# Two graph layers over 64 graphs: a step table of its own for the first four graphs, turns on PE for graph 1 and the last two transitions, and weight sums on POOL

## The chip, the cores and the metric

The kernel runs on one core of one Trainium2 chip. The metric is the device time of one execution in microseconds (us); lower is better. Most executions of a kernel here lie within 5 us of each other. A run is called fast when it is not over 1.5% above the fastest of its kernel; here that is every run that could be judged. A profile of one execution gives each engine's instructions: PE (matmuls), DVE (vector), ACT (scalar), POOL (GpSimd) and SP, whose queue issues the DMAs.

## The reference, cut to what matters

Each of 64 graphs has 256 nodes with 512 features and a 256 x 256 adjacency.

```python
def reference(x, adj, W, Wv, bv, aw, ab, Wk, bk):            # names shortened
    h = relu(layernorm(x))                                    # layer 0
    agg = einsum('bij,bjf->bif', adj, h) / max(sum(adj, -1), EPS)
    x = x + relu(concat([h, agg], 2) @ W.T)
    h = relu(layernorm(x))                                    # layer 1
    Xw = h @ Wv + bv
    e = leaky_relu((Xw @ aw[:d])[:, None, :] + (Xw @ aw[d:])[:, :, None] + ab, 0.2)
    t = adj * exp(e);  t = t / sum(t, -1)                     # the "transition"
    H = 0; Xk = h
    for k in range(3):
        H = H + Xk @ Wk[k] + bk[k];  Xk = t @ Xk
    return x + relu(H)
```

## The kernel before

A matrix is turned (transposed) before it can be PE's stationary operand. In the kernel before, that goes through DRAM: 32 x 32 blocks are turned on DVE, four DMAs put them into DRAM, one fetches them. A product of 256 x 512 x 1024 is done in seven block products (Strassen's way), so the weights need sums t1 to t4, and each turned h needs four block sums on POOL. One graph passes through these pieces: `prepare` (norm, turn of h and adj), `layer0`, `turn1` (norm, turn of h), `own` and `pair` (seven products each), `transition`, `twice`. A table fixes the order in which the pieces of neighbouring graphs are interleaved; each letter is one step of a piece, and each engine executes its instructions in that order.

```python
def blocks(ht, pool, name, bufs=1):                           # four sums on POOL
    ...
    nc.gpsimd.tensor_add(s1, a21, a22); nc.gpsimd.tensor_sub(s2, s1, a11)
    nc.gpsimd.tensor_sub(s3, a11, a21); nc.gpsimd.tensor_sub(s4, a12, s2)

def seven(a, b, banks, width, name, c12, c22, ...):           # each add: 2 matmuls, 4 PE records
    add(p, a11, b["b11"], True);  nc.scalar.copy(r, p);              yield
    add(p, s2, b["t2"]);  nc.scalar.copy(d, p); nc.scalar.copy(m16, p);  yield
    ...
    add(p, s4, b["b22"]); nc.vector.tensor_add(c12, p, m16);         yield

def first(sp, spp):                    # graph 0 alone: turned on PE, then all of W, then its adj
    ...
    H0T[0] = blocks(flipped_on_pe(h, F, early, spp, "h0t"), early, "h0t")
    weights_l0(w0_sb, sp, spp)
    ANT[0] = flipped_on_pe(scaled(A[0]), N, early, spp, "ant")

TURN = ("EWU NL NEU mUIWL ... MOP")    # for every graph g: L layer0(g), N prepare(g+1), M/m turn1,
                                       # O own(g-1), P pair(g-2), E transition(g-2), U twice(g-3), W weights
LAST = "mEU UE UO ... V"               # the last three graphs
```

## Time and profile before

| what | value |
|---|---|
| time, median of 6 fast runs | 2654.9 us |
| span of the profiled run | 2653.9 us |
| PE busy | 98% |
| PE wait from 120 to 2600 us | none |
| PE waits before 120 us / after 2600 us | 36.4 us / 3.3 us |

Read it so: the middle runs at PE's pitch, so only the two ends can give anything. The lines that say so stand in the prediction. Two more lines from the groups by shape of the kernel before matter later; after the bar they give busy time and the mean of one in ns:

```profile
L219 POOL TENSOR_TENSOR h1t_s<-h1t_s,h1t 128x256 f32<-128x256 f32 x64 | 74.1, 1158 | 5.0
L219 POOL TENSOR_TENSOR h0t_s<-h0t_s,h0t 128x256 f32<-128x256 f32 x64 | 47.7, 745 | 5.0
L184 DVE SCALAR_TENSOR_TENSOR nmr<-mv,rstd 128x2 f32<-128x2 f32 x128 | 53.1, 415 | 103.7 <-POOL rstd L181 103.7
```

The same POOL sum of the same size takes 1158 ns on average in one place and 745 in another. A DVE operation on two numbers per partition (`nmr`), which takes 0.16 us wherever it runs alone, has a mean of 0.415.

### The profile page before, as it was taken

The numbers are of one execution on the slowest core, as the hardware profiler recorded it, in microseconds if no ns is written. First come the engines' busy times: TensorE is split into PE (matmuls) and PEld (weight loads), VectorE is DVE, ScalarE is ACT, GpSimd is POOL, SyncE is SP. The second block draws the span as 40 slices with busy tenths as digits, with TensorE's granted clock in tenths as the row PEclk, the third lists the DMA queues.
The fourth block names the chain that finished last, engine by engine and source line by source line (L and its number), as shares of the span: only waits on it lengthen the run. The fifth ranks groups of instructions, "written<-read, shape, count | busy, mean of one in ns | idle before, by whom it ended". The sixth has DMA issues, their size and how long they took to land.

```text
span 2653.9 us, 23482 instructions
## 1 busy us (share of the span) xinstructions
PE 2609.8 (98%) x6961; PEld 1346.0 (51%) x6962; DVE 1204.9 (45%) x2670; ACT 895.7 (34%) x1803; POOL 509.6 (19%) x780
## 2 busy tenths in 40 slices
PE   6899999999999999999999999999999999999998
PEld 3455555545555555555455455555555554555554
DVE  5544444444444444444444444444444444444433
ACT  2233333333333333333333333333333333333332
POOL 1221122112112111211221121122112112211210
PEclk8999999999999999999999999999999999999999
DMA  6444453444444444444435444444444454444432
GB/s 188 120 122 106 119 117 103 121 120 105 121 109 113 119 112 113 123 101 123 115 103 121 117 110 117 111 112 121 110 114 123 98 124 118 103 121 110 108 75 58
DMA packets 582942, 301.55 MB, mean 114 GB/s; under 512 B 424224, under 2 KB 547360, under 8 KB 582816
## 3 DMA queue, kind: packets, MB, share of 16 engines
q1 hardware_dynamic: 582816, 300.06, 45.9%
q8 instruction: 56, 0.92, 0.1%
q14 instruction: 70, 0.57, 0.1%
HBM read 166.46 MB, written 133.50 MB: 113 GB/s over the span
## 4 chain that ended last, share of the span: by engine, by line
PE 97%; DMA 1%; DVE 1%; ACT 0%; issue 0%; SPq 0%; POOL 0%; DVEq 0%; ACTq 0%; POOLq 0%
PE bank L225 96%; DMA h0t<-dh0t 0%; SPq L205 0%; DMA row<-ds 0%; DMA tt<-dtt 0%; PE tr L103 0%; DVE turned L200 0%; DMA ds<-sj 0%; DMA z<-in_L_gnn_bv_dram 0%; DMA x<-in_x_dram 0%; DVE stats L174 0%; ACT h L186 0%; PE tr L116 0%; DMA dh1t<-turned 0%; PE bank L467 0%
## 5 line engine op out<-in xcount | busy, mean ns | idle before, releaser
L225 PE MATMUL bank<-l_t,h0t_s 128*128 128x512 f32 x768 | 362.4, 595 | 4.2 <-ACT bank L237 4.2
L225 PE MATMUL bank<-l_t,h1t_s 128*128 128x512 f32 x768 | 360.6, 592 | 0.7 <-ACT bank L237 0.7
L237 ACT COPY bank<-bank 128x512 f32<-128x512 f32 (+1 forms) x192 | 95.9, 499 | 714.4 <-PE bank L225 714.4
L200 DVE STREAM_TRANSPOSE turned<-h 128x512 f32<-128x512 f32 x254 | 180.3, 710 | 312.8 <-ACT h L186 311.9
L218 POOL TENSOR_TENSOR h0t_s<-h0t 128x256 f32<-128x256 f32 x64 | 54.2, 847 | 1032.7 <-DMA h0t<-dh0t 936.1
L225 PE MATMUL bank<-l_b,h0t 128*128 128x512 f32 x512 | 243.8, 599 | 6.0 <-DMA h0t<-dh0t 5.3
L225 PE MATMUL bank<-q,tt 128*128 128x512 f32 x512 | 240.2, 592 | 2.6 <-DMA tt<-dtt 2.6
L225 PEld LDWEIGHTS bank<-l_t,h0t_s 128*128 128x128 f32 x768 | 146.2, 191 | 189.2 <-issue 174.3
L225 PE MATMUL bank<-l_b,h1t 128*128 128x512 f32 x512 | 240.5, 592 | 0.0
L225 PE MATMUL bank<-u,tt 128*128 128x512 f32 x512 | 240.4, 592 | 0.0
L225 PE MATMUL bank<-q,ant 128*128 128x512 f32 x512 | 230.2, 592 | 0.0
L179 POOL TENSOR_SCALAR ve<-mv 128x2 f32<-128x2 f32 x128 | 28.3, 221 | 1005.6 <-DVE mv L175 1005.4
L186 ACT ACTIVATE h<-x,nmr,rstd 128x512 f32<-128x512 f32 x256 | 202.4, 818 | 31.5 <-DVE nmr L184 29.6
L225 PE MATMUL bank<-l1s_t,h1t_s 128*128 128x258 f32 x768 | 198.6, 381 | 0.5 <-ACT bank L237 0.5
L225 PEld LDWEIGHTS bank<-l_t,h1t_s 128*128 128x128 f32 x768 | 145.0, 189 | 104.8 <-issue 92.7
L225 PEld LDWEIGHTS bank<-l1s_t,h1t_s 128*128 128x128 f32 x768 | 146.3, 191 | 102.0 <-issue 83.9
L317 DVE SCALAR_TENSOR_TENSOR x<-bank,x 128x512 f32<-128x512 f32 x128 | 88.3, 691 | 195.2 <-PE bank L225 195.2
L253 DVE TENSOR_TENSOR q<-bank,m 128x512 f32<-128x512 f32 x128 | 88.5, 691 | 191.6 <-PE bank L225 190.6
L174 DVE BATCH_NORM_STATS2 stats<-x 128x6 f32<-128x512 f32 x256 | 172.0, 672 | 5.1 <-DMA x<-in_x_dram 5.1
L225 PEld LDWEIGHTS bank<-l_b,h0t 128*128 128x128 f32 x512 | 101.5, 199 | 127.8 <-issue 120.3
L225 PEld LDWEIGHTS bank<-q,tt 128*128 128x128 f32 x512 | 100.5, 196 | 122.5 <-issue 112.3
L225 PEld LDWEIGHTS bank<-q,ant 128*128 128x128 f32 x512 | 100.4, 196 | 119.4 <-issue 110.3
(100 smaller groups left out, 3228.6 us busy)
## 6 DMA issues: line engine op xcount, KB each, us to landing
x<-in_x_dram SPq DMA_DIRECT2D x64, 512.0 KB, 5.5
dh1t<-turned SPq DMA_DIRECT2D x256, 128.0 KB, 2.8
h1t<-dh1t SPq DMA_DIRECT2D x64, 512.0 KB, 3.9
out_dram<-o SPq DMA_DIRECT2D x64, 512.0 KB, 3.2
dh0t<-turned SPq DMA_DIRECT2D x252, 128.0 KB, 2.8
h0t<-dh0t SPq DMA_DIRECT2D x63, 512.0 KB, 4.2
a<-in_adj_dram SPq DMA_DIRECT2D x64, 256.0 KB, 3.2
dtt<-turned SPq DMA_DIRECT2D x256, 64.0 KB, 3.3
```

The source lines that it names most:

```text
L174: nc.vector.bn_stats(stats[:, c, :], src[:, c, :])
L179: nc.gpsimd.tensor_scalar(ve, mv[:, :, 1], LN_EPS, None, op0=ALU.add)
L186: nc.scalar.activation(to[:, c, :], src[:, c, :], AF.Relu, bias=nmr[:, c : c + 1], scale=rstd[:, c : c + 1])
L200: nc.vector.transpose(self.turned.rearrange("p b r c -> p c b r")[:, c], src.rearrange("p c (b s) -> p c b s", s=Q)[:, c])
L218: nc.gpsimd.tensor_add(s1, a21, a22)
L225: nc.tensor.matmul(ps, lhs, rhs, start=start, stop=stop, skip_group_check=True)
L237: nc.scalar.copy(r, p)
L253: nc.vector.tensor_add(c22, p, m167)
L317: nc.vector.scalar_tensor_tensor(x1[:, c, :], banks0[1 + c], 0.0, x[:, c, :], op0=ALU.max, op1=ALU.add)
```

## The change

Its intent is to fill PE's idle start. Graphs 0 and 1 enter side by side, in banks of their own, both turned on PE (`second` is new); the first four graphs have a table `FIRST`; layer 1's weights are loaded and summed within it; some weight sums move from DVE to POOL. At the end, the last two transitions are turned on PE in place of DRAM.

```diff
-    def combine(b, b12):
-        nc.vector.tensor_sub(b["t1"], b12, b["b11"]) ...            # t1, t2, t3, t4 on DVE
+    def combine(b, b12, eng=(nc.vector,) * 4):
+        for e, to, x, y in zip(eng, ("t3", "t1", "t2", "t4"), ...):
+            e.tensor_sub(b[to], ...)
 ...
+        sums = combine(B1, b12, (nc.gpsimd,) * 4)                   # layer 1
         for c in range(FC):
+            next(sums)
             for s in range(2):
                 nc.vector.scalar_tensor_tensor(scr, wv_sb[c // 2][:, c % 2, :], 1.0, aw_sb[:, s, :], ...
 ...
-    def transition(g):
+    def transition(g, tr_banks=None):
 ...
+        if tr_banks:
+            TT[g] = flipped_on_pe(t, N, tr_banks, work, "tt")
+        else:
             flip = Flip(N, "tt") ...
 ...
+        sums = combine(B0, b12, (nc.gpsimd,) + (nc.vector,) * 3)    # layer 0: t3 on POOL
+        for _ in range(3):
+            next(sums)
+        yield
+        next(sums)
+        yield
+        ANT[0] = flipped_on_pe(scaled(A[0]), N, tr_banks, early, "ant")
+    def second(tr_banks):
+        h = yield from norm_relu(X[1])
+        t = flipped_on_pe(h, F, tr_banks, work, "h1t", 2)
+        yield
+        H0T[1] = blocks(t, work, "h1t", 2)
+        yield
+        ANT[1] = flipped_on_pe(scaled(A[1]), N, tr_banks, early, "ant")
 ...
-    TURN = ("EWU NL NEU mUIWL ...
+    TURN = "EU NL NEU mUIL ...                                      # the same without W
+    FIRST = ("F IIWWA SSA FA SSA FSSA QB QA B QA QQB A QQA ISB aB aQWB QaWB QaWaB WB "
+        "aQWIC bWC bWRC aC bWRaC bWC bWC "
+        "bIORC bROPC ROP RcOP RcbOP RcOP RcOOE cRP cRP "
+        "EDo cDo NEEDo EENDo cEDo NEDo NDoo eNEDk INeDk EdeNzU deNU eUkU kUdk dkNeUkp NeNp edkIp Nep dIp dp p ")
-    LAST = "mEU UE UO UO U UO P O EEP O EEP O EEP OOO eP E eP P u ue ueu eu uep ep ep ep ep p p V V V V V V"
+    LAST = "mEU UE UO UO U UO EEP O EEP O EP OEP OOO eP eP P u uee ue ue u ue up ep p p p p p V V V V V V"
```

More of the change, by code (lines that the diff above doesn't have):

```diff
@@ L1 @@
+import itertools
 from contextlib import ExitStack
@@ L58, in gnn_two_layers @@
     small = ctx.enter_context(tc.tile_pool(name="small", bufs=4))
+    work = ctx.enter_context(tc.tile_pool(name="work", bufs=1))
+    psum = ctx.enter_context(tc.tile_pool(name="psum", bufs=1, space=bass.MemoryType.PSUM))
+    banks0 = [psum.tile([P, F], FP, name=f"bank0_{i}") for i in range(3)]
+    banks1 = [psum.tile([P, F], FP, name=f"bank1_{i}") for i in range(3)]
+    banks2 = [psum.tile([P, F], FP, name=f"bank2_{i}") for i in range(2)]
     dram = ctx.enter_context(tc.tile_pool(name="dram", bufs=2, space=bass.MemoryType.DRAM))
@@ L82, in gnn_two_layers @@
     zero = const.tile([P, F], BF, name="zero")
-    def combine(b, b12):
-        nc.vector.tensor_sub(b["t1"], b12, b["b11"])
-        yield
-        nc.vector.tensor_sub(b["t2"], b["b22"], b["t1"])
-        yield
-        nc.vector.tensor_sub(b["t3"], b["b22"], b12)
-        yield
-        nc.vector.tensor_sub(b["t4"], b["b21"], b["t2"])
-        yield
-    def weights_l0(w0_sb, sp, spp):
-        b12 = sp.tile([P, FC // 2, F], FP, name="l0_b12")
-        for oc in range(FC):
-            for side in range(2):
-                pt = spp.tile([P, FC, P], FP, name="tr")
-                for k in range(FC):
-                    kc = side * FC + k
-                    nc.tensor.transpose(pt[:, k, :], w0_sb[oc][:, kc * P : (kc + 1) * P], ident)
-                put = nc.scalar.copy if side else nc.vector.tensor_copy
-                for kh, to in enumerate((b12, B0["b22"]) if side else (B0["b11"], B0["b21"])):
-                    put(to[:, :, oc * P : (oc + 1) * P], pt[:, 2 * kh : 2 * kh + 2, :])
-        for _ in combine(B0, b12):
-            pass
@@ L110, in flipped_on_pe, with turned_on_pe @@
-    def flipped_on_pe(src, width, pool, spp, name):
-        t = pool.tile([P, width // P, P, NC], FP, name=name, bufs=1)
+    def combine(b, b12, eng=(nc.vector,) * 4):
+        for e, to, x, y in zip(eng, ("t3", "t1", "t2", "t4"), ("b22", None, "b22", "b21"), (None, "b11", "t1", "t2")):
+            e.tensor_sub(b[to], b12 if x is None else b[x], b12 if y is None else b[y])
+            yield
+    def turned_on_pe(blocks, banks):
+        for i in range(0, len(blocks), FC):
+            pt = next(banks).rearrange("p (k n) -> p k n", k=FC)
+            for k, block in enumerate(blocks[i : i + FC]):
+                nc.tensor.transpose(pt[:, k, :], block, ident)
+            yield pt
@@ new lines, in weights_l0 @@
+    def weights_l0(w0_sb, b12, banks):
+        for side, to in enumerate(((B0["b11"], B0["b21"]), (b12, B0["b22"]))):
+            pts = turned_on_pe([w0_sb[oc][:, (side * FC + k) * P :][:, :P] for oc in range(FC) for k in range(FC)], banks)
+            for oc, pt in enumerate(pts):
+                for kh in range(2):
+                    (nc.scalar.copy if oc % 2 else nc.vector.tensor_copy)(to[kh][:, :, oc * P : (oc + 1) * P],
+                                                                         pt[:, 2 * kh : 2 * kh + 2, :])
@@ L113, in flipped_on_pe @@
+    def flipped_on_pe(src, width, banks, pool, name, bufs=1):
+        t = pool.tile([P, width // P, P, NC], FP, name=name, bufs=bufs)
         for c in range(NC):
-            pt = spp.tile([P, FC, P], FP, name="tr")
-            for k in range(width // P):
-                nc.tensor.transpose(pt[:, k, :], src[:, c, k * P : (k + 1) * P], ident)
-            (nc.scalar.copy if c else nc.vector.tensor_copy)(t[:, :, :, c], pt[:, : width // P, :])
-        return t
+            for pt in turned_on_pe([src[:, c, k * P : (k + 1) * P] for k in range(width // P)], banks):
+                (nc.scalar.copy if c else nc.vector.tensor_copy)(t[:, :, :, c], pt[:, : width // P, :])
+        return t
@@ L120, in weights_l1, with spare @@
+    def spare(name, bufs=1):
+        return work.tile([P, 2, F], FP, name=name, bufs=bufs).rearrange("p s f -> p (s f)")
     def weights_l1():
-        aw_sb, *wv_sb, b12 = (work.tile([P, 2, F], FP, name=n, bufs=3 if n == "x1" else 1) for n in ("x1", "u", "o", "q1"))
-        b12s = work.tile([P, NC, 2, HW], FP, name="e", bufs=2).rearrange("p c s w -> p (c s) w")[:, : FC // 2, :]
+        aw_sb = spare("x1", 4).rearrange("p (s f) -> p s f", s=2)
+        wv_sb = [work.tile([P, NC, 2, HW], FP, name="e", bufs=2).rearrange("p c s w -> p (c s w)")[:, : 2 * F]
+                 .rearrange("p (c f) -> p c f", c=2) for _ in range(2)]
+        b12s = spare("u")[:, : FC // 2 * HW].rearrange("p (c w) -> p c w", w=HW)
+        b12 = spare("o").rearrange("p (c f) -> p c f", f=F)
@@ L126, in weights_l1 @@
         scr, bv_sb = (work.tile([P, F], FP, name=n) for n in ("z0", "z1"))
-        biases = [work.tile([P, F], FP, name=n) for n in ("m16_1", "m167_1", "tt")]
+        two = work.tile([P, FC, P, NC], FP, name="h1t", bufs=2).rearrange("p k n c -> p (k n c)")
+        biases = [two[:, :F], two[:, F:], work.tile([P, F], FP, name="tt")]
         vc = small.tile([P, 2, FC], FP, name="vc", bufs=1)
@@ L131, in weights_l1 @@
         src = [wk[k].rearrange("(h c p) o -> h p c o", p=P, h=2) for k in range(NW)]
-        nc.sync.dma_start(aw_sb.rearrange("p s f -> p (s f)"), bcast(aw, 0, 2 * F))
+        nc.sync.dma_start(aw_sb, bcast(aw, 0, 2 * F))
         for h in range(2):
             nc.sync.dma_start(wv_sb[h], wv.rearrange("(h c p) o -> h p c o", p=P, h=2)[h])
-        yield
         halves = ((b12s, 0, 1), (B2["b22"], 1, 1), (B2["b11"], 0, 0), (B2["b21"], 1, 0))
@@ L142, in weights_l1 @@
             nc.sync.dma_start(to, src[k][kh])
+        nc.sync.dma_start(bv_sb, bcast(bv, 0, F))
+        nc.sync.dma_start(ab_sb, bcast(ab, 0, 1))
+        for k in range(NW):
+            nc.sync.dma_start(biases[k], bcast(bk, k * F, F))
         yield
+        sums = combine(B1, b12, (nc.gpsimd,) * 4)
         for c in range(FC):
+            next(sums)
             for s in range(2):
@@ L150, in weights_l1 @@
             nc.vector.tensor_copy(to[:, :, half], vc[:, col, 2 * kh : 2 * kh + 2])
-        yield
         yield from combine(B2, b12s)
-        nc.sync.dma_start(bv_sb, bcast(bv, 0, F))
-        nc.sync.dma_start(ab_sb, bcast(ab, 0, 1))
-        for k in range(NW):
-            nc.sync.dma_start(biases[k], bcast(bk, k * F, F))
-        yield
         for s in range(2):
@@ L161, in weights_l1 @@
         nc.vector.scalar_tensor_tensor(c0, cc[:, 0:1], cc[:, 1:2], ab_sb, op0=ALU.add, op1=ALU.add)
-        yield
-        yield from combine(B1, b12)
         nc.vector.tensor_add(bk_sb, biases[0], biases[1])
@@ L166, in weights_l1, with finished, norm_relu @@
         yield
-    def norm_relu(src, to):
+    def finished(steps):
+        while True:
+            try:
+                next(steps)
+            except StopIteration as end:
+                return end.value
+    def norm_relu(src):
         stats = small.tile([P, NC, 6], FP, name="stats")
@@ L184, in norm_relu @@
         nc.vector.scalar_tensor_tensor(nmr, mv[:, :, 0], -1.0, rstd, op0=ALU.mult, op1=ALU.mult)
+        h = early.tile([P, NC, F], FP, name="h", bufs=1)
         for c in range(NC):
-            nc.scalar.activation(to[:, c, :], src[:, c, :], AF.Relu, bias=nmr[:, c : c + 1],
+            nc.scalar.activation(h[:, c, :], src[:, c, :], AF.Relu, bias=nmr[:, c : c + 1],
                                  scale=rstd[:, c : c + 1])
             yield
+        return h
     class Flip:
@@ L284, in prepare @@
     def prepare(g):
-        h = early.tile([P, NC, F], FP, name="h", bufs=1)
-        yield from norm_relu(X[g], h)
+        h = yield from norm_relu(X[g])
         flip = Flip(F, "h0t")
@@ L305, in prepare, with layer0 @@
         yield
-    def layer0(g):
-        q = work.tile([P, NC, F], FP, name="q0")
-        yield from seven(H0T.pop(g), B0, banks0, F, "0", q[:, 0, :], q[:, 1, :])
-        steps = spread(banks0[1:], ANT.pop(g), q)
+    def layer0(g, banks=None, name="0"):
+        banks = banks or banks0
+        q = work.tile([P, NC, F], FP, name=f"q{name}")
+        yield from seven(H0T.pop(g), B0, banks, F, name, q[:, 0, :], q[:, 1, :])
+        steps = spread(banks[1:], ANT.pop(g), q)
         next(steps)
@@ L314, in layer0 @@
         next(steps)
-        x, x1 = X.pop(g), work.tile([P, NC, F], FP, name="x1", bufs=3)
+        x, x1 = X.pop(g), work.tile([P, NC, F], FP, name="x1", bufs=4)
         for c in range(NC):
-            nc.vector.scalar_tensor_tensor(x1[:, c, :], banks0[1 + c], 0.0, x[:, c, :], op0=ALU.max, op1=ALU.add)
+            nc.vector.scalar_tensor_tensor(x1[:, c, :], banks[1 + c], 0.0, x[:, c, :], op0=ALU.max, op1=ALU.add)
         X1[g] = x1
@@ L321, in turn1 @@
     def turn1(g):
-        h = early.tile([P, NC, F], FP, name="h", bufs=1)
-        yield from norm_relu(X1[g], h)
+        h = yield from norm_relu(X1[g])
         flip = Flip(F, "h1t")
@@ L334, in turn1, with own @@
         yield
-    def own(g):
+    def own(g, p=None):
         e = E[g] = work.tile([P, NC, 2, HW], FP, name="e", bufs=2)
-        yield from seven(H1T[g], B2, [banks0[0]] + banks2, HW, "s", e[:, 0, 1, :], e[:, 1, 1, :],
+        yield from seven(H1T[g], B2, [p or banks0[0]] + banks2, HW, "s", e[:, 0, 1, :], e[:, 1, 1, :],
                          e[:, 0, 0, :], e[:, 1, 0, :])
@@ L380, in transition @@
         yield
-        flip = Flip(N, "tt")
-        flip.turn(t)
-        flip.put()
-        yield
-        TT[g] = flip.get(work)
+        if tr_banks:
+            TT[g] = flipped_on_pe(t, N, tr_banks, work, "tt")
+        else:
+            flip = Flip(N, "tt")
+            flip.turn(t)
+            flip.put()
+            yield
+            TT[g] = flip.get(work)
         yield
@@ L424, in loads_of, with set_bits, first @@
             yield
-    def first(sp, spp):
+    def set_bits(banks):
+        for bank in banks:
+            nc.tensor.matmul(bank, zero[:, :P], zero, start=True, stop=True)
+    def first(tr_banks):
         load(0, X)
-        w0_sb = [sp.tile([P, 2 * F], FP, name=f"w0_sb{oc}") for oc in range(FC)]
+        w0_sb = [spare(*n) for n in (("x1", 4), ("q1",), ("u",), ("o",))]
         for oc in range(FC):
             nc.sync.dma_start(w0_sb[oc], w0[oc * P : (oc + 1) * P, :])
-        load(0, A)
-        for what in (X, A):
-            load(1, what)
+        for g, what in ((1, X), (0, A), (1, A)):
+            load(g, what)
         make_identity(nc, ident)
@@ L437, in first @@
         nc.gpsimd.memset(zero, 0.0)
-        h = early.tile([P, NC, F], FP, name="h", bufs=1)
-        for _ in norm_relu(X[0], h):
-            pass
-        H0T[0] = blocks(flipped_on_pe(h, F, early, spp, "h0t"), early, "h0t")
-        weights_l0(w0_sb, sp, spp)
-        ANT[0] = flipped_on_pe(scaled(A[0]), N, early, spp, "ant")
-    TURN = ("EWU NL NEU mUIWL NL NNU NEL EWNU EUL ENL ENL EWP WNL L IO MP MO MP WO MP EMO NMP WO WP O WO MOP")
-    LAST = "mEU UE UO UO U UO P O EEP O EEP O EEP OOO eP E eP P u ue ueu eu uep ep ep ep ep p p V V V V V V"
+        set_bits(banks0[1:] + banks1[1:])
+        h = finished(norm_relu(X[0]))
+        H0T[0] = blocks(flipped_on_pe(h, F, tr_banks, early, "h0t"), early, "h0t")
+        b12 = spare("q0").rearrange("p (c f) -> p c f", f=F)
+        weights_l0(w0_sb, b12, tr_banks)
+        sums = combine(B0, b12, (nc.gpsimd,) + (nc.vector,) * 3)
[5 more added lines that the diff above has]
+        ANT[0] = flipped_on_pe(scaled(A[0]), N, tr_banks, early, "ant")
+        yield
+    def second(tr_banks):
+        h = yield from norm_relu(X[1])
+        t = flipped_on_pe(h, F, tr_banks, work, "h1t", 2)
+        yield
+        H0T[1] = blocks(t, work, "h1t", 2)
+        yield
+        ANT[1] = flipped_on_pe(scaled(A[1]), N, tr_banks, early, "ant")
+        set_bits(banks2)
+        yield
+    TURN = "EU NL NEU mUIL NL NNU NEL ENU EUL ENL ENL EP NL L IO MP MO MP O MP EMO NMP O P O O MOP"
+    FIRST = (
+        "F IIWWA SSA FA SSA FSSA QB QA B QA QQB A QQA ISB aB aQWB QaWB QaWaB WB "
+        "aQWIC bWC bWRC aC bWRaC bWC bWC "
+        "bIORC bROPC ROP RcOP RcbOP RcOP RcOOE cRP cRP "
+        "EDo cDo NEEDo EENDo cEDo NEDo NDoo eNEDk INeDk EdeNzU deNU eUkU kUdk dkNeUkp NeNp edkIp Nep dIp dp p "
+    )
+    LAST = "mEU UE UO UO U UO EEP O EEP O EP OEP OOO eP eP P u uee ue ue u ue up ep p p p p p V V V V V V"
     def run(order, pieces):
@@ L457, in gnn_two_layers @@
     with tc.manual_schedule(engines={getattr(mybir.EngineType, e) for e in ("PE", "DVE", "Activation", "Pool", "SP")}):
-        with tc.tile_pool(name="setup", bufs=1) as sp, \
-                tc.tile_pool(name="setup_ps", bufs=3, space=bass.MemoryType.PSUM) as spp:
-            first(sp, spp)
-        work = ctx.enter_context(tc.tile_pool(name="work", bufs=1))
-        psum = ctx.enter_context(tc.tile_pool(name="psum", bufs=1, space=bass.MemoryType.PSUM))
-        banks0 = [psum.tile([P, F], FP, name=f"bank0_{i}") for i in range(3)]
@@ L464, in gnn_two_layers @@
-        banks1 = [psum.tile([P, F], FP, name=f"bank1_{i}") for i in range(3)]
-        banks2 = [psum.tile([P, F], FP, name=f"bank2_{i}") for i in range(2)]
-        for bank in banks0[1:] + banks1[1:] + banks2:
-            nc.tensor.matmul(bank, zero[:, :P], zero, start=True, stop=True)
-        norms, w = {}, weights_l1()
-        for g in range(G):
-            norms[g] = turn1(g)
-            run(TURN, {"I": loads_of(g + 2) if g + 2 < G else iter(()), "N": prepare(g + 1) if g + 1 < G else iter(()),
-                       "L": layer0(g), "M": norms[g], "W": w,
-                       **({"m": norms.pop(g - 1), "O": own(g - 1)} if g > 0 else {}),
-                       **({"E": transition(g - 2), "P": pair(g - 2)} if g > 1 else {}),
-                       **({"U": twice(g - 3)} if g > 2 else {})})
@@ L476, in gnn_two_layers @@
-        run(LAST, {"m": norms.pop(G - 1), "U": twice(G - 3), "E": transition(G - 2), "P": pair(G - 2),
-                   "O": own(G - 1), "u": twice(G - 2), "e": transition(G - 1), "p": pair(G - 1), "V": twice(G - 1)})
+        norms = {g: turn1(g) for g in range(G)}
+        tr_banks = itertools.cycle([banks1[0], *banks2])
+        run(FIRST, {"F": first(tr_banks), "S": second(itertools.cycle(banks2)), "W": weights_l1(),
+                    "I": itertools.chain(*map(loads_of, range(2, 6))), "A": layer0(0), "B": layer0(1, banks1, "1"),
+                    "z": map(set_bits, [[banks1[0]]]), "C": layer0(2), "D": layer0(3), "Q": prepare(2), "R": prepare(3), "N": prepare(4),
+                    "a": norms[0], "b": norms[1], "c": norms[2], "d": norms[3], "O": own(0), "o": own(1, banks1[0]),
+                    "k": own(2), "P": pair(0), "p": pair(1), "E": transition(0), "e": transition(1), "U": twice(0)})
@@ new lines, in gnn_two_layers @@
+        for g in range(4, G):
+            run(TURN, {"I": loads_of(g + 2) if g + 2 < G else iter(()), "N": prepare(g + 1) if g + 1 < G else iter(()),
+                       "L": layer0(g), "M": norms[g], "m": norms[g - 1], "O": own(g - 1), "E": transition(g - 2),
+                       "P": pair(g - 2), "U": twice(g - 3)})
+        tr_banks = itertools.cycle(banks0[1:])
+        run(LAST, {"m": norms[G - 1], "U": twice(G - 3), "E": transition(G - 2, tr_banks), "P": pair(G - 2),
+                   "O": own(G - 1), "u": twice(G - 2), "e": transition(G - 1, tr_banks), "p": pair(G - 1),
+                   "V": twice(G - 1)})
```

## The prediction

> **What bounds the kernel now.** I read the page's busy table and slices first, then busy time by stretches, then the waits of PE, then the chain at the two ends.
>
> ```profile
> span 2653.9 us, 23482 instructions
> PE 2609.8 (98%) x6961; PEld 1346.0 (51%) x6962; DVE 1204.9 (45%) x2670; ACT 895.7 (34%) x1803; POOL 509.6 (19%) x780
> PE   6899999999999999999999999999999999999998
> PEclk8999999999999999999999999999999999999999
> ```
>
> PE is full in all slices but the first two and the last, and the granted clock dips only at the start. The stretches say where the missing time lies:
>
> ```profile
> core 0: us, PE busy (x) PEld busy (x) DVE busy (x) ACT busy (x) POOL busy (x), PEclk, DMA share, GB/s
> 0.00:40.00 40.00, 22.61 (x77) 13.58 (x79) 16.92 (x34) 11.86 (x23) 6.07 (x20) 0.91 0.59 187
> 40.00:80.00 40.00, 28.92 (x65) 13.46 (x63) 23.16 (x56) 7.10 (x13) 12.17 (x16) 0.83 0.68 194
> 80.00:120.00 40.00, 32.12 (x76) 15.89 (x77) 22.56 (x47) 14.38 (x29) 8.46 (x14) 0.87 0.41 103
> 160.00:2500.00 2340.00, 2340.00 (x6249) 1207.79 (x6249) 1068.61 (x2375) 803.55 (x1618) 458.71 (x694) 1.00 0.47 114
> 2600.00:2654.00 54.00, 46.12 (x118) 21.89 (x116) 0.98 0.19 51
> ```
>
> From 120 us to 2600 us PE never waits. A busy PE need not be a fast one, so I also take its pitch, from start to start:
>
> ```profile
> 107.97 3.60 PE L225 MATMUL bank<-q,ant 128*128 128x512 f32 x8
> 111.40 1.03 PE L225 MATMUL bank<-l1s_b,h1t 128*128 128x258 f32 x4
> 112.28 1.02 PE L225 MATMUL bank<-l_t,h1t_s 128*128 128x512 f32 x2
> ```
>
> (111.40 - 107.97) / 8 = 0.429 us for a record 512 wide, (112.28 - 111.40) / 4 = 0.22 for one 258 wide (0.2175 with more digits of other rows). Each f32 matmul leaves two records. The groups by form count 5120 and 1792 of them, so 80 and 28 a graph: 34.3 + 6.1 = 40.4 us a graph, 64 x 40.43 = 2587 us in all. The span is 67 us longer. In the first 120 us the groups hold 124 wide and 44 narrow records, 62.8 us of work: 57.2 us are lost there. The last 54 us lose about 8; the two sum to the 67, nearly. The 57.2 consist of 36.4 us of waits, 10.5 of setup on PE (transposes of graph 0 and the weights, and the matmuls that set the banks' bits) and about 10.4 of matmuls at a reduced clock (73.3 us busy for 62.8 of work). The waits, longest first:
>
> ```profile
> PE tr L116 <- ACT h L186: 9.0, 1, 9.0
> PE bank L225 <- ACT m_s L250: 7.0, 1, 7.0
> PE tr L116 <- ACT an L281: 6.9, 1, 6.9
> PE bank L225 <- DMA h0t<-dh0t: 5.3, 1, 5.3
> PE bank L225 <- ACT bank L237: 4.7, 4, 2.6
> PE bank L225 <- ACT m L250: 2.2, 1, 2.2
> ```
>
> The first 9.0 is the load of x and its norm. The others come from graphs entering one by one: each pass through layer 0, norm, turn in DRAM, load back is serial, and there is no other graph's work for PE. At the tail the chain shows one such wait:
>
> ```profile
> 2613.15 0.72 DVE turned L200
> 2615.25 1.83 DMA dtt<-turned
> 2617.17 5.04 DMA tt<-dtt
> 2622.26 8.97 PE bank L225 x20
> 2631.25 0.58 ACT bank L237
> ```
>
> PE had finished pair of graph 62 at 2619.64 and waited 2.62 us for its turned transition; a bank copy cost another 0.66.
>
> **What the Trainium skill says.** "TensorE: Matmul & The Clock Gate", Part 1: after an idle window of about 3.4 us the PE clock falls to half, and about 3.4 us of sustained work restores it. The trace agrees in kind: after the wait of 5.3 us the next four 512-wide records took 3.78 us instead of 1.88, and the granted clock stayed at 0.50 until about 61 us. After a wait of only 2.24 us, at 101 us, it fell too, a few us later. Part 4 of the same page says a PE transpose gives a full 128x128 turn, lands in PSUM and so needs a copy, and does not count as busy for the clock; the trace has 32 of them in 5.23 us, 0.163 each, and cannot decide on the clock. "DMA: Bandwidth & Descriptors", section "Anatomy of one DMA", gives about 2 us fixed per transfer, mostly the receipt of the last byte (fitted on the GpSimd path). Here four 64 KB puts land in 3.3 us (median) and the 256 KB load in 2.7, or 5.04 at the tail, so a turn through DRAM costs 5 to 9 us. "GPSIMD Engine Reference", "Engine selection", calls elementwise work with two inputs about 2x slower there than on DVE: 0.74 us for 256 elements on POOL against 1.23 for 1024 on DVE agrees, so about 2.9 us (estimate) for a POOL sum of 1024.
>
> **The change part by part.** The built order shows that the repeated table is the old one without the weights' steps; the matmuls of the 64 graphs are the same. The middle should stay at 40.43 us a graph; everything is decided at the ends.
>
> *Start to layer 0.* Load, norm and the 40 transposes keep their times, so PE is at 16.0 us. The turn of adj 0 moves from before layer 0 into it, so the first product starts at 16.0 instead of 26.95. It runs to 17.9; the second needs t2. The weights' copies end at 16.7, then t1 and t2 at 1.23 each: 19.2. t3 went to POOL (16.7 to 19.6) and is not awaited. Products 2, 3, 4 (1.72 each) end at 24.3.
>
> *adj 0 and graph 1 on PE.* DVE does stats of x1, t4, nmr and deg by 23.4; ACT scales adj by 26.0. PE waits about 1.3 us; 12 small turns and their copies through two banks hold it to 28.2. Then six products, three of each graph by turns, so that the copies of one lie under the products of the other, and the spread of graph 0: 6 x 1.72 + 3.43 = 13.7, PE at 41.9.
>
> *adj 1.* DVE reaches deg of adj 1 only after x1 of graph 0, which needs that spread. x1 1.3, deg and reciprocal 1.1, ACT 0.5: the first turn at 44.5. Turns, copies and two bit-setting matmuls: layer 0 of graph 1 resumes at 46.8. By then PE has done ten products and one spread, 17.2 + 3.4 = 20.6: 26.2 us lost. The kernel before ended the same work at about 61.8, with 41.2 lost.
>
> *The rest of the table.* Four products and a spread of graph 1 end at 57.1. Graph 2's turned h went out at about 39 and is back near 50, so it waits for no DMA. Its block sums stand on POOL behind two weight sums of 2.9, so the second product waits about 1.5, and layer 0 of graph 2 ends at 57.1 + 12.0 + 1.5 = 70.6. Own of graph 0 needs its turned h1: h at 57, turned on DVE by 61.7 among the weights' sums, out and in by 71 to 73: 1.5 of wait. Then 21.5 us of own 0, pair 0 and spread 2 and 18.1 of layer 0 of graph 3 with own 1 run without a long wait. Graph 0's transition (sj near 91, row near 102, tt near 118 to 119) meets PE at 118: 1 us. The single pair of graph 1 and the u copies: about 1.3. Sum: 26.2 + 1.5 + 1.5 + 1 + 1.3 = 31.5 us lost to waits, setup and turns.
>
> *Clock.* The first products come after transposes and 2 us of waits, and the hole at 42 to 45 is 3 us: two dips of 3.4 to 7 us at half clock would cost 1.7 to 3.4 each; with part of it under waits I take 3.5 (estimate). Head: 35 us lost against 57.2, so 22 us gained.
>
> *Tail.* Removed: 2.62, and most of the 0.66. Added: 8 transposes, 8 x 0.163 = 1.3. And a new place to wait: PE now reaches the turn of graph 63 near 2629, while the row of sj came at 2626.4, and exp, max, sums and scale took 6.2 us after it. Without the other DMAs the row may come a us or two earlier; I take 1.2 of wait. Net 0.5 us.
>
> Sum: 2655.0 - 22 - 0.5 = 2632.5; I say 2632.
>
> **The rivals.** (a) *Graph 1 starves the weights and flips*: the loads of layer 1's weights now follow x 2 and adj 2 and one reuses the buffer of w0, so it is issued only after 16 us; SP issues in order. 4 MB at the 300 GB/s of the first 40 us is there by 35. For it: DVE is 58% busy in the second stretch already and runs in order. If DVE sums and norms lag 10 us, the gain falls to 12: 2643. (b) *The clock*: if transposes leave PE at half clock until 24 us and each of the small waits trips it, 5 us more: 2637. (c) *All holes filled better than my walk*: only 16 of start, 6 of turns and 4 of copies remain, 26 lost: 2623. (d) *The handover to the repeated table is out of phase* and it waits every graph: 0.5 us each would be 30, back to 2662. The same order ran 2480 us without a wait, so I give this a few per cent.
>
> **Range and chances.** (a) to (c) span 2623 to 2643, the range for 8 in 10. Faster by over 2% would need below 2603, a loss of 6 us in the head, when the first product cannot start before 16: 1%. Slower by over 2% needs (d) doubled: 1%.
>
> **What would show it.** First layer-0 product near 16 us; a PE wait of about 3 us near 42 for adj 1; no wait for h0t from DRAM; full slices from about 125 us with the same pitch; at the tail no wait for tt and a short one before the turn of graph 63. Wrong if waits of PE remain in the middle, if the first 160 us still hold over 50 us of loss, or if the clock is below 0.8 over most of the first 60.

## The result, and the profile after

The changed kernel takes 2643.5 us (median of 6), the one before 2654.9. The ratio is 0.9959, 95% interval 0.9946 to 0.9972: faster, by 11.4 us, well inside 2%. (Ratios here are the mean time of one kernel's fast runs over that of the other's fast runs of the same rounds, so not quite the ratio of the medians quoted.) The predicted time was 2632, with a range of 2623 to 2643; the measured one lies just above it, and the gain is half of the predicted one. The profiled execution is the slowest of the changed kernel's six, 1.9 us above their median, so its trace shows a little less gain than the median does.

The busy table and slices of the changed kernel:

```profile
span 2643.6 us, 23486 instructions
PE 2612.3 (99%) x6983; PEld 1347.6 (51%) x6983; DVE 1204.4 (46%) x2664; ACT 897.2 (34%) x1807; POOL 524.2 (20%) x785
PE   7999999999999999999999999999999999999999
PEclk9999999999999999999999999999999999999999
```

The first stretches, with the columns shown of before (busy us of PE, PEld, DVE, ACT, POOL, then the granted clock):

```profile
0.00:40.00 40.00, 28.33 (x92) 16.27 (x93) 17.17 (x33) 13.29 (x26) 13.81 (x27) 0.96 0.70 256
40.00:80.00 40.00, 31.46 (x67) 13.32 (x67) 31.25 (x59) 9.23 (x16) 17.82 (x14) 0.87 0.35 81
80.00:120.00 40.00, 37.94 (x113) 21.26 (x112) 19.14 (x48) 14.44 (x32) 12.77 (x20) 1.00 0.54 114
120.00:160.00 40.00, 35.80 (x97) 18.75 (x97) 17.01 (x40) 11.86 (x25) 5.10 (x8) 0.96 0.50 122
```

PE is fuller, but from 40 to 80 us it still misses 8.5 us, and DVE is now busy 31.25 of 40 there (some of this will turn out to be waiting). From 160 us on PE never waits until the tail, at the old pitch. What PE waited for (total, times, longest):

```profile
PE bank L240 <- DVE q L275: 7.4, 2, 5.3
PE bank L101 <- ACT h L200: 5.2, 1, 5.2
PE bank L101 <- ACT an L296: 3.5, 2, 2.4
PE bank L240 <- DVE l_t L93: 3.4, 1, 3.4
PE bank L240 <- ACT u L425: 2.3, 1, 2.3
```

Gone are the 9.0 (in part: PE now sets bank bits during the load of x), the 7.0, the 6.9 and the 5.3 for a turn through DRAM. In their place DVE holds PE, for a sum `q` (5.3 and 2.1 us) and for layer 0's weight sum t2 (3.4). The longest wait for each of these, and the one for u's copies, are followed by four records that take 3.6 to 3.8 us in place of 1.88, which is half clock:

```profile
21.69 3.58 PE L240 MATMUL bank<-l_t,h0t_s 128*128 128x512 f32 x4 [3.37 <-DVE l_t L93]
65.04 3.78 PE L240 MATMUL bank<-q,ant 128*128 128x512 f32 x4 [5.30 <-DVE q L275]
137.80 3.57 PE L240 MATMUL bank<-u,tt 128*128 128x512 f32 x4 [2.28 <-ACT u L425]
```

The reason that DVE is late is seen when DVE and POOL are laid side by side. In DVE's order of time (start, length):

```profile
17.05 1.22 DVE L93 TENSOR_TENSOR l_t<-q,l_b 128x1024 f32<-128x1024 f32 x1 [0.28 <-ACT q L110]
18.37 3.17 DVE L93 TENSOR_TENSOR l_t<-l_b,l_t 128x1024 f32<-128x1024 f32 x1
57.40 2.75 DVE L159 SCALAR_TENSOR_TENSOR z<-e,x 128x512 f32<-128x512 f32 x1
60.09 2.28 DVE L197 SCALAR_TENSOR_TENSOR nmr<-mv,rstd 128x2 f32<-128x2 f32 x1
64.31 0.68 DVE L275 TENSOR_TENSOR q<-bank,m 128x512 f32<-128x512 f32 x1
```

And in POOL's:

```profile
17.36 3.10 POOL L93 TENSOR_TENSOR l_t<-l_b,q 128x1024 f32<-128x1024 f32 x1 [2.77 <-ACT l_b L110]
57.25 2.35 POOL L93 TENSOR_TENSOR l_t<-l_b,o 128x1024 f32<-128x1024 f32 x1
59.56 2.79 POOL L93 TENSOR_TENSOR l_t<-o,l_b 128x1024 f32<-128x1024 f32 x1
63.91 1.06 POOL L234 TENSOR_TENSOR h0t_s<-h0t_s,h0t 128x256 f32<-128x256 f32 x1
```

t1 and t2 on DVE are the same operation on the same size: 1.22 us and 3.17. POOL's t3 ends at 17.36 + 3.10 = 20.46; t2 ends 1.08 us after that, as if it had started only then. DVE's product at 57.40 ends 0.55 us after POOL's sum at 57.25 does, and `nmr` at 60.09, otherwise 0.16 us, ends at 62.37, just behind POOL's second sum (62.35). But `q<-bank,m` at 64.31, with one operand in PSUM, takes its usual 0.68 under a POOL sum. So the theory formed: an operation of DVE with two SBUF inputs and one of POOL that reads SBUF exclude each other for their whole length. The Trainium skill says just that, in "SBUF — State Buffer", section "SBUF: two separate sides": the port pair that both share is "an exclusive lock, not a bandwidth split". The prediction had not looked it up.

### The profile page after: what moved, and what is told of

Its sections match the earlier page's. It is cut to its first block, busy times and chain, and to the rows that moved or that the text cites. A ratio compares the mean times of both kernels' runs of the same rounds, so it can differ in the third digit from the quotient of the medians.

```text
span 2643.6 us, 23486 instructions
## 1 busy us (share of the span) xinstructions
PE 2612.3 (99%) x6983; PEld 1347.6 (51%) x6983; DVE 1204.4 (46%) x2664; ACT 897.2 (34%) x1807; POOL 524.2 (20%) x785
## 4 chain that ended last, share of the span: by engine, by line
PE 97%; DVE 1%; issue 0%; ACT 0%; DMA 0%; SPq 0%; POOL 0%; DVEq 0%; ACTq 0%
PE bank L240 97%; PE bank L101 0%; DVE z L159 0%; DVE l_t L93 0%; DMA x<-in_x_dram 0%; DMA row<-ds 0%; DVE turned L215 0%; SPq L220 0%; DVE stats L187 0%; ACT z L377 0%; DVE nmr L197 0%; DVE o L433 0%; ACT an L296 0%; DVE l1s_t L93 0%; POOL rstd L194 0%
## 5 line engine op out<-in xcount | busy, mean ns | idle before, releaser
L240 PE MATMUL bank<-l_t,h1t_s 128*128 128x512 f32 x780 | 367.4, 594 | 0.7 <-ACT bank L252 0.7
L240 PE MATMUL bank<-l_t,h0t_s 128*128 128x512 f32 x756 | 356.9, 595 | 4.1 <-DVE l_t L93 3.4
L240 PE MATMUL bank<-l_b,h0t 128*128 128x512 f32 x504 | 237.2, 593 | 0.0
L240 PEld LDWEIGHTS bank<-u,tt 128*128 128x128 f32 x512 | 100.6, 197 | 121.5 <-issue 88.4
```

The lines of the kernel that those rows point to most:

```text
L240: nc.tensor.matmul(ps, lhs, rhs, start=start, stop=stop, skip_group_check=True)
```

## The experiments

The theory is that the blocking by POOL's sums makes DVE late and that this cost the missing part of the gain. The main rival: DVE is just loaded with too much in the order of the table, and the long operations are a sign and not the cause. Others: the hole for adj 1; the u copies on ACT; the tail. Twelve kernels ran, each beside the kernel before on the same chip.

| run | edits to the changed kernel | us, median | before | ratio | 95% interval |
|---|---|---|---|---|---|
| after_again | none | 2642.8 | 2655.2 | 0.9955 | 0.9943 to 0.9968 |
| t3_on_dve | t3 on DVE | 2644.5 | 2656.5 | 0.9955 | 0.9940 to 0.9970 |
| l1_sums_early | layer 1's POOL sums at 37 us | 2640.0 | 2656.5 | 0.9941 | 0.9927 to 0.9956 |
| l1_sums_on_dve | layer 1's sums on DVE | 2643.6 | 2656.5 | 0.9952 | 0.9935 to 0.9968 |
| adj1_early | scaling of adj 1 earlier | 2640.9 | 2656.5 | 0.9944 | 0.9929 to 0.9959 |
| all_three | t3_on_dve, l1_sums_early and adj1_early | 2634.2 | 2654.2 | 0.9924 | 0.9909 to 0.9939 |
| u_copy_first | u's copies ahead on ACT | 2640.5 | 2654.2 | 0.9948 | 0.9933 to 0.9963 |
| tail_as_before | old tail | 2643.6 | 2654.2 | 0.9961 | 0.9946 to 0.9976 |
| best1 | all_three, u_copy_first, weight products earlier | 2630.9 | 2654.2 | 0.9913 | 0.9897 to 0.9930 |
| unblocked | t3_on_dve and l1_sums_early | 2640.1 | 2655.2 | 0.9940 | 0.9927 to 0.9952 |
| l1_blank | memsets for sums (wrong result) | 2639.0, one run | 2655.2 | - | - |
| best2 | best1, bias sums later | 2628.6 | 2655.2 | 0.9899 | 0.9884 to 0.9914 |

A single edit is worth little more than the spread.

**t3_on_dve.**

```diff
-        sums = combine(B0, b12, (nc.gpsimd,) + (nc.vector,) * 3)
+        sums = combine(B0, b12)                     # rows in the order t1, t2, t3, t4
```

> The changed kernel with one edit: layer 0's weight sum t3 goes from POOL to DVE, behind t1 and t2. Theory (POOL and DVE block each other when both read two SBUF operands): DVE's sum t2, 3.17 us in the changed kernel, is 1.22 again, the second product starts at 19.6 us instead of 21.7 and the wait of 3.37 before it is about 1.3; 2643.5 becomes about 2641.5. Rival (t2 is late because its data come late, and the sum just ran beside much DMA traffic): t2 stays above 2.5 us and the time stays or grows by the 1.2 us of the added DVE sum, 2643 to 2645.

In the trace t2 is 1.21 us again, the second product's wait is 1.42 and it starts at 19.78 us, not 21.69: the theory's half of the expectation holds. The time did not fall, 2644.5. The trace shows why. ACT's scaling of adj 0 is waited for longer (1.93 us, not 1.08), but since the second product now runs at full clock, the lead is still 2.7 us when the turn of adj 0 begins (27.09 us, not 29.80). It is 1.0 us at the product after that (32.38, not 33.40), because the turns of graph 1 and the product behind them now run at half clock:

```profile
28.05 1.57 PE L104 MATMUL bank<-ident,h 128*128 128x128 f32 x8
29.41 3.14 PE L243 MATMUL bank<-l_t,h0t_s 128*128 128x512 f32 x4
```

In the changed kernel these take 1.09 and 1.88 us. The lead is 0.8 us at 64, and own of graph 0 starts at 83.86 instead of 84.22.

**l1_sums_early.** DVE's order and load are untouched; only POOL's sums move, to where POOL was idle.

```diff
-        sums = combine(B1, b12, (nc.gpsimd,) * 4)
+        for _ in combine(B1, b12, (nc.gpsimd,) * 4):
+            pass
+        yield
         for c in range(FC):
-            next(sums)
-        "... FSSA QB QA B QA ..."
+        "... FSSA QB QA W B QA ..."
```

> The changed kernel with one edit: the four weight sums of layer 1 stay on POOL but stand where DVE has no operation with two SBUF inputs (POOL is idle from 37 to 56 us). DVE's order and load are untouched. Theory (blocking): the products for aw on DVE are 0.69 us each instead of 1.31 on average, nmr 0.16 instead of 2.28, PE's wait of 5.30 before the second half of graph 1's spread falls to about 1 and the later one of 2.06 to under 0.5; with less half clock, 2643.5 becomes 2634 to 2637. Rival (DVE is simply loaded with the weights' sums in the order of the table): the waits stay within 1 us of 5.3 and 2.06, the time within 1.5 us of 2643.5.

The same two places of DVE in this kernel's order of time, then PE's wait for `q`:

```profile
57.07 0.69 DVE L160 SCALAR_TENSOR_TENSOR z<-e,x 128x512 f32<-128x512 f32 x1
57.69 0.15 DVE L198 SCALAR_TENSOR_TENSOR nmr<-mv,rstd 128x2 f32<-128x2 f32 x1
```

```profile
59.89 1.99 PE L241 MATMUL bank<-q,ant 128*128 128x512 f32 x4 [0.49 <-DVE q L276]
```

The product is 0.69 us, not 2.75; `nmr` 0.15, not 2.28; PE's wait 0.49, not 5.30, and no half clock follows it. The rival falls for this wait, since DVE's order did not change. The time fell to 2640.0, 3 us short of what was expected. The wait before own of graph 0 did not shrink as expected (2.40 us, since DVE's bias sums stand in front of `q`, as best2 will show), and the waits for tt (1.72) and for u's copies (2.72) grew. Counted from the first product (16.03 us here, 16.44 in the changed kernel), own of graph 0 starts 5.5 us earlier, the second product of graph 1's pair only 4.1 us.

The new place is not as free as the expectation says. Two operations of DVE still wait for POOL's sums there, and the second has only one input in SBUF:

```profile
36.74 2.30 DVE L198 SCALAR_TENSOR_TENSOR nmr<-mv,rstd 128x2 f32<-128x2 f32 x1 [1.13 <-POOL rstd L195]
42.61 1.20 DVE L293 TENSOR_SCALAR deg<-deg 128x2 f32<-128x2 f32 x1
```

Elsewhere they take 0.16 and 0.17 us.

**l1_sums_on_dve.**

```diff
-        sums = combine(B1, b12, (nc.gpsimd,) * 4)
+        sums = combine(B1, b12)
```

> The changed kernel with one edit: the four weight sums of layer 1 run on DVE, at the same places of the table, as in the kernel before. Theory (blocking): before the sum q that PE waits for, DVE gains two sums of 1.22 and loses about 4.85 of blocking, so PE's wait of 5.30 falls to about 2.9; 2643.5 becomes 2640 to 2642. Rival (load of DVE): the two sums are added to the load, the wait grows to about 7.7 and the time to 2645 to 2648.

PE's wait for `q` was 2.71 us: it shrank although DVE got more work, so the blocking cost DVE more than the sums themselves. The time stayed at 2643.6, not the 2640 to 2642 expected. In the trace the other waits for `q` took back half of the 2.6 us (2.61 us before own of graph 0 where the changed kernel has 2.06, and a new one of 0.78), and a product behind them ran at half clock (3.46 us for 1.88, at 83.87). This is the kernel before's choice, and it is no better.

**l1_blank.** A wrong result on purpose (relative error 0.18).

```diff
-        sums = combine(B1, b12, (nc.gpsimd,) * 4)
+        def blank():
+            for to in ("t3", "t1", "t2", "t4"):
+                nc.gpsimd.memset(B1[to], 0.0)
+                nc.gpsimd.memset(B1[to], 0.0)
+                yield
+        sums = blank()
```

> The changed kernel with a wrong result on purpose: in the places of the four POOL sums of layer 1 stand pairs of memsets on POOL of the same targets, which write SBUF and read nothing. If it is the reading of SBUF by both engines that blocks, DVE's products beside them are 0.69 us each and PE's wait of 5.30 is near 1. If any POOL instruction of that length blocks DVE, products beside them stay above 1.3 us and the wait above 3.

DVE and POOL side by side in this kernel:

```profile
57.61 0.69 DVE L164 SCALAR_TENSOR_TENSOR z<-e,x 128x512 f32<-128x512 f32 x1
```

```profile
56.99 0.95 POOL L158 MEMSET l_t<- 128x1024 f32 x1
57.88 0.95 POOL L157 MEMSET l_t<- 128x1024 f32 x1
```

The eight products average 0.679 us and PE waits 0.49. POOL is at work beside the products here too (two memsets of 0.95 us for each sum of 2.35), but with instructions that only write: for DVE's operations with two SBUF inputs it is the reading that blocks. Memsets are not harmless to all of DVE: of its copies of two numbers from SBUF to SBUF behind the products, which take 0.155 us alone, two took 0.98 and 1.60 and ended with POOL's memset at 65.9 us.

**unblocked and after_again.** Both edits for the blocking together, beside the changed kernel itself.

> The changed kernel itself, unaltered, beside the others on the same chip: 2642 to 2645. It sets the scale for the three below, since single runs of one kernel spread by 3 us.

> The changed kernel with both POOL edits (t3 on DVE, layer 1's sums early on POOL), all else as it is: what the blocking costs in all. Theory: the sum of what the two edits gave alone, 3.5 to 5 us, so 2638.5 to 2640; DVE's products 0.69, t2 1.22. Rival (the two hide each other, because own of graph 0 hangs on graph 0's transposes through DRAM): no more than layer 1's sums early alone, and the wait for DVE's q before own of graph 0 grows instead.

2640.1 against 2642.8. The intervals of the ratios overlap, as they share the noise of the kernel before; but the five runs of unblocked (2637.1 to 2641.5) all lie below the five of the changed kernel (2642.0 to 2645.8), and the means differ by 4.2 us. It is no more than l1_sums_early gave alone (ratio 0.9940 against 0.9941), as the rival said. The traces show where it goes. In unblocked own of graph 0 starts at 76.46 us instead of 83.45, and the second product of graph 1's pair comes at 143.71 instead of 147.19. Counted from each run's first product (15.33 and 15.97 us, before any edit acts), the blocking costs 6.4 us where it acts, and 2.8 are left 70 us later. First after_again, then unblocked:

```profile
83.45 1.15 PE L240 MATMUL bank<-l1s_b,h1t 128*128 128x258 f32 x4 [2.06 <-DVE q L275]
84.43 1.88 PE L240 MATMUL bank<-q,ant 128*128 128x512 f32 x4
137.57 1.99 PE L240 MATMUL bank<-u,tt 128*128 128x512 f32 x4 [2.58 <-ACT u L425]
```

```profile
76.46 1.15 PE L244 MATMUL bank<-l1s_b,h1t 128*128 128x258 f32 x4 [2.40 <-DVE q L279]
77.44 3.25 PE L244 MATMUL bank<-q,ant 128*128 128x512 f32 x4
132.42 3.66 PE L244 MATMUL bank<-u,tt 128*128 128x512 f32 x4 [2.88 <-ACT u L429]
```

Both have the same two waits, 0.3 us longer in unblocked. But there each is followed by half clock (3.25 and 3.66 us, not 1.88 and 1.99), which takes most of the 3.5 us that were given back.

**adj1_early.**

```diff
         H0T[1] = blocks(t, work, "h1t", 2)
+        an = scaled(A[1])
         yield
-        ANT[1] = flipped_on_pe(scaled(A[1]), N, tr_banks, early, "ant")
+        ANT[1] = flipped_on_pe(an, N, tr_banks, early, "ant")
```

> The changed kernel with one edit: degree and scaling of adj 1 stand before the norm of graph 2 and the residual of graph 0, where DVE and ACT are idle (32 to 35 us). My walk had a hole there that hangs on DVE's order: the turn of adj 1 then starts right after the spread of graph 0, the wait of 2.37 us vanishes. If nothing downstream hangs on PE here, 2643.5 becomes about 2641; if the time regained is only waited for later, because the spread of graph 1 waits for DVE's sum q anyway, that wait grows by as much and the time stays within 1 us of 2643.5.

The wait of 2.37 us is gone (0.68 remains before the bank bits are set), own of graph 0 starts at 80.34, and the time is 2640.9, as expected. This hole was in the prediction and measured as predicted; it shows only what the table left.

**u_copy_first.**

```diff
-        "... EdeNzU deNU eUkU kUdk dkNeUkp ..."
+        "... EdNzU dNU eUkeU kUdk dkNeeUkp ..."
```

> The changed kernel with one edit: the two copies of u of graph 0 stand on ACT ahead of the exponentials of graph 1, which wait for their row from DRAM. If u's copies were late only because of ACT's order, the wait of 2.28 us at 137.8 and the half clock after it vanish: 2 to 4 us less, about 2640.5. If PE depends on the row anyway soon after, the wait turns up at the next product of graph 1 (q times tt) and the time stays within 1.5 us of 2643.5.

The wait and the half clock behind it vanish, 2640.5. In the changed kernel ACT's exponentials of graph 1, which their row from DRAM lets start only at 134.71 us, and two scalings stood in front of u's copies in ACT's order, up to 137.18, while PE had finished the spread at about 134.5.

**tail_as_before.** The old `LAST`, and both calls of `transition` without `tr_banks`.

> The changed kernel with its last table and its two last transitions as they were in the kernel before (turned through DRAM). It tells the tail's share of the gain: the traces put it at 1.4 us (51.27 us from the first tail product to the last in the kernel before, 49.86 in the changed one). Expected 2644 to 2646, with a wait of 2.6 us for tt back in the tail. My prediction had 0.5.

2643.6, slightly below the range: no difference shows in the time. In the trace the wait for tt is back (2.35 us), and from the first of these tail products to the last the tail takes 51.01 us, against 49.86 in the changed kernel. The turns on PE are worth about 1.2 us, which the run-to-run spread hides. In the changed kernel they are these; the second set was waited for 0.17 us:

```profile
2603.14 0.60 PE L101 MATMUL bank<-ident,an 128*128 128x128 f32 x4
2620.75 0.84 PE L101 MATMUL bank<-ident,an 128*128 128x128 f32 x4 [0.17 <-ACT an L393]
```

**all_three, best1, best2.** First the three edits t3_on_dve, l1_sums_early and adj1_early together; then also u_copy_first, with three pairs of weight products moved into a time when DVE was idle; then the bias sums behind the `q` that own of graph 0 waits for.

```diff
-        "... ISB aB aQWB QaWB QaWaB WB aQWIC bWC bWRC aC bWRaC bWC bWC bIORC bROPC ROP ..."
+        "... ISB aWWWB aQWB QaB QaaB B aQWIC bWC bWRC aC bWRaC bWC bWC bIORC bROPC ROP ..."    # best1
+        "... ISB aWWWB aQWB QaB QaaB B aQWIC bWC bWRC aC bWRaC bC bC bIORC bROPWC ROP ..."     # best2
```

> The changed kernel with the three edits together: t3 on DVE, layer 1's POOL sums early, adj 1 early. Alone they moved the start of own of graph 0 from 84.2 us to 83.9, 78.3 and 80.3. If the head is one chain on which these times stand one behind the other, it starts near 74 and the time falls to 2634 to 2637. If another chain takes over behind them (transition of graph 0 and the row of graph 1, which end in waits for tt and for u's copy), the head's gain is eaten by longer waits there (over 2 us for tt, over 3 us for u) and the time is 2637 to 2640.

> A version meant to beat both: the three edits, u's copies first, and three of the four pairs of weight products on DVE moved to where DVE waited idle (49 to 54 us). If the waits are what the head loses, 2643.5 becomes 2630 to 2635, which is where the prediction had put the change itself; if the transition of graph 0 bounds the head, it stays at 2636 to 2640.

> best1 with one more edit: the bias sums on DVE (3.3 us) stand behind the sum q that own of graph 0 waits for (2.13 us in best1). If that wait was only DVE's order, it falls under 0.7 and the time is 1 to 2 us below best1, near 2629.5. If own of graph 0 waits next for its turned h1 or its block sums, the time stays at 2630 to 2632.

All three are correct and their times fall within what was expected or just below it: own of graph 0 starts at 73.46, 72.93 and 71.97 us. The wait before it falls from 2.13 us in best1 to 0.78 in best2 (under 0.7 was expected), so that wait was DVE's order. best2 beats both kernels, 2628.6 us, 26.6 below the kernel before and 14 below the changed one. PE's waits in its first 160 us, longest in total first:

```profile
PE bank L104 <- ACT h L204: 4.8, 1, 4.8
PE bank L104 <- ACT an L300: 1.9, 1, 1.9
PE bank L244 <- DMA h0t<-dh0t: 1.9, 1, 1.9
PE bank L449 <- POOL zero L461: 1.9, 1, 1.9
```

DVE is no longer among the first; what is left is the load of x and small things.

## Why the prediction was right or wrong

Its frame held. The middle kept its pitch and had no waits; the gain came from the start; it was below 2%; the first product began at 16.44 us, "near 16"; the hole for adj 1 was there (2.37 us, predicted near 3). That graph 2 waited for no DMA before its layer 0 was luck: its turned h was issued at 58.86 us and back 4.0 us later, not near 50, and only since PE itself came late (68.6 us, not 57.1) was it not waited for. best1 and best2, where PE is earlier, wait 1.9 us for it. The size was wrong. The head gained 2594.44 - 2585.60 = 8.8 us (the place of the same first tail product in the two traces) where 22 were predicted, so it loses 57.2 - 8.8 = 48.4 us and not 35. The walk against the trace:

| place | predicted us | measured us | late by |
|---|---|---|---|
| first product | 16.0 | 16.44 | 0.4 |
| second product | 19.2 | 21.69 | 2.5 |
| spread of graph 0 ends | 41.9 | 45.4 | 3.5 |
| layer 0 of graph 1 resumes | 46.8 | 49.70 | 2.9 |
| spread of graph 1 ends | 57.1 | 68.6 | 11.5 |
| own of graph 0 starts | 72.1 | 84.22 | 12.1 |
| graph 0's transition meets PE | 118 | 130.9, after 1.3 of wait | 12.9 |

The step that failed is the durations of DVE and POOL where they run together. "t1 and t2 at 1.23 each: 19.2" took each engine's operation at its length alone; beside POOL's t3, t2 took 3.17. "Four products and a spread of graph 1 end at 57.1" assumed that DVE's `q` comes when PE has finished; it came 5.3 us late, of which the early sums and the memsets show 4.8 to be blocking (0.49 is left without it). The prediction did price the POOL sums, "about 2.9 us (estimate)" for 2.35 measured without a collision, and let a product wait for POOL behind two of them; that they stop DVE was not in it. unblocked puts this step, with the half clock that it brings, at 6.4 us at own of graph 0, of the 12.1, and at 4.2 us of the time, of the 11.5 missing. So it is the largest single step and not the whole. Term by term, the 13.4 us that the head loses beyond the prediction in this trace are: 7.4 at the two places where DVE was late (3.37 us of wait for 1.3, 5.30 for none), 3.1 of half clock, 1.6 at u's copies and the wait of 0.66 us behind them, and about 1.3 in small terms of both signs.

A second term was mis-sized: "The single pair of graph 1 and the u copies: about 1.3" measured 2.28 + 0.66 us of wait and 1.7 more at half clock (four records in 3.57 us instead of 1.88; in after_again none). It does not go with the blocking: the wait is 2.58 us in after_again and 2.88 in unblocked; ACT's order sets it, as u_copy_first shows.

The third is the clock, which was added as 3.5 us and not set into the walk. Three times before own of graph 0 matmuls ran slow: the second product 3.58 for 1.88, the products at 49.7 us 4.89 for 3.60, the spread at 65.04 3.78 for 1.88; 4.9 us, with 1.7 more for u: 6.6 for 3.5. In this trace a wait of 2.3 to 5.3 us brought 1.3 to 1.9 more with it, so a mis-sized wait costs more than itself. Rival (b) fell in its first half, since the first product ran at full speed (1.89 us at 16.44); its second half, that the waits trip the clock, is what happened, at 3.1 us for the 5 it named.

Rival (a), DVE lagging, was nearest: 2643. It was right in its outcome, mostly by luck: its reason, late loads and DVE's share of work in order, is shown only for the wait before own of graph 0 (2.1 us, 0.8 in best2). For the wait of 5.3 it is not: l1_sums_early had the same DVE order and hardly waited for that `q`. Rival (c) was not reached; best2, with 2628.6, is 5.6 us above it. In the tail 0.5 us were predicted and 1.2 to 1.4 found; the wait for graph 63's turn was 0.17 us and not 1.2.

Three readings of the prediction were loose, without consequence for the result. The terms that it names from own of graph 0 to the transition give 111.7 us and not 118; a spread of graph 3 and two products of own of graph 2 (5.2 us) are left out of them, though not out of the table above. The "300 GB/s of the first 40 us" is 187 in its own lines. And the transposes of the kernel before could have decided on the clock: their records last 421 ns at first and 273 later.

What stays open: how much of the half clock after the waits belongs to an edit and how much to the single execution that was profiled. Executions of one kernel differ here. In the trace of tail_as_before the second product ran at full speed after the same wait of 3.37 us, and in after_again the u product did after 2.58 us; each is worth 1.7 us.

## What to carry to other kernels

Moving an operation to an idle engine is free only if the engines share nothing: before giving POOL a sum over SBUF, list which DVE operations run beside it. Beside POOL's sums, DVE's sums from PSUM (0.68 us), its turns (0.70) and its reductions (0.65) kept their length here. Those with two SBUF inputs waited, and so did, with one SBUF input, a TENSOR_SCALAR on two numbers (1.20 us for 0.17); small copies waited even beside memsets. In a profile, look for a small operation whose mean is far above its minimum (0.415 us for 0.16 in the kernel before): it may be waiting inside its own bar, where no wait is listed. And when a start-up is one chain, part of the gain of one hole filled is taken back by the next wait, so fill them together and judge each by the trace.

## What the Trainium skill lacked or had wrong

- "SBUF — State Buffer", section "SBUF: two separate sides", has the exclusive lock, and the runs agree with it, also that a POOL instruction which reads no SBUF leaves DVE's two-input operation alone (0.679 us beside memsets, up to 2.75 beside sums). It does not say how it looks in a profile: the blocked instruction counts as busy for the whole wait (a 0.16 us operation shown as 2.28), and no wait is listed.
- "TensorE: Matmul & The Clock Gate", Part 4, says transposes do not count as busy for the clock. In the changed kernel PE did nothing but f32 transposes from 8.95 us on, and their pitch went from 0.213 us (12.42 to 13.27, four of them) to 0.108 (14.87 to 15.30); the product after them ran at full speed. The pitch is the only sign, as the granted clock is recorded as 1.00 all through this stretch. The start of each group of four is the first column:

```profile
12.42 1.06 PE L101 MATMUL bank<-ident,u 128*128 128x128 f32 x4
13.27 1.06 PE L101 MATMUL bank<-ident,o 128*128 128x128 f32 x4
14.87 0.60 PE L101 MATMUL bank<-ident,q 128*128 128x128 f32 x4
15.30 0.60 PE L101 MATMUL bank<-ident,u 128*128 128x128 f32 x4
```

- The same page, Part 1, puts the limit at an idle window of about 3.4 us. Here waits well under that were followed by half clock too. Of the ten traces with a wait for u's copies (2.28 to 2.88 us), six have half clock after it (3.39 to 3.66 us for 1.88, the shortest wait among them) and four have not (1.99). For planning, such a wait is better priced with 1.5 to 1.8 us more, as a chance of about six in ten (an estimate from these ten).
